# AUGRU from step 88 on with both halves as one

## The chip, the cores and the metric

The kernel runs on one core of a Trainium2 chip. The metric is the device time of one execution in microseconds, as the median of several runs. Engines are named as in the profile: PE (TensorE) multiplies matrices, PEld is its loading of weights, DVE (VectorE), ACT (ScalarE), POOL (GpSimd), and SP issues most of the transfers.

## The reference

A model of a recommender for 1024 users with a history of 100 items, 128 numbers each. A first GRU runs over the history, attention over its states gives weights, and a second GRU with an attention gate (AUGRU) runs over the same states. A small network then scores the user. All is float32.

```python
def augru_step(h, inp):
    x_t, a_t = inp                      # state of the first GRU, attention weight
    ti = jnp.concatenate([h, x_t], axis=-1)
    r = jax.nn.sigmoid(ti @ aug_Wr.T + aug_br)
    u = jax.nn.sigmoid(ti @ aug_Wu.T + aug_bu)
    h_hat = jnp.tanh(jnp.concatenate([h * r, x_t], axis=-1) @ aug_Wh.T + aug_bh)
    u = a_t[:, None] * u
    h_new = (1.0 - u) * h + u * h_hat
    return (h_new, h_new)
_, aug_seq = jax.lax.scan(augru_step, h0, (jnp.swapaxes(keys, 0, 1), att_seq))
...
idx = (sequential_length - 1)[:, None, None]   # lengths 1 to 100
attention_feature = jnp.take_along_axis(aug_out, idx, axis=1)[:, 0, :]
comb = jnp.concatenate([user, item, hist_sum, item * hist_sum, attention_feature], axis=1)
scores = _mlp(comb, layers, jax.nn.sigmoid)    # 640 -> 200 -> 80 -> 1
```

Only the state at a user's own last step is used, so a user whose history has ended need not be carried on.

## The kernel before

The first phase (GRU, attention, pooling) takes about 1400 us and is not touched. Users are then sorted by length, longest first, and dealt out to two halves of 512 columns (`NH = 2`, `HB = 512`). A state is held as 128 features by columns. In the second phase (`augru_phase`) step t works on the first `widths[t]` columns of each half alone: a planned bound on the users still alive (`ALIVE`), but never under `LEAST`, which is 96. The program holds this phase three times, for three plans of widths; a number computed on the chip chooses one. With the inputs here it is the first, whose bound falls from 512 to 14 columns: 100 at step 82, 96 at 83, 90, 86, 80, 76 at 84 to 87, then 70, 64, 60, 54, 50, 44, 40, 34, 28, 24, 18, 14. So before the change all steps from 83 on have 96 columns in each half.

The order of all engines' work is written out by hand (`manual_schedule`); each engine takes its instructions in that order. The two halves alternate: `half_step(t, i)` does one step of one half, and while one half waits for its gates the other fills the engines.

- `open_gates` starts the three sums of the next half step, `pr`, `ph` and `pu`, with their products with the key (the first GRU's state, L1110). `close_gate` ends each with its second product: `pr` and `pu` with the state `h`, `ph` with `r` (L1114). Each product appears in the profile as two MATMUL instructions with a weight load each.
- ACT makes the sigmoids of `pr` and `pu` in place (L1134, L1135) and the tanh of `ph` into `c` (L1122).
- DVE makes `r = h * pr` (L1140), `pu = pu * at` (L1148, `at` is the row of attention weights, the same in all partitions), `rest = (pu - 1) * h` (L1151), `pu = pu * c` (L1138) and the new state `h = pu - rest` (L1142). It also transposes the keys of two steps ahead in blocks of 32 columns (L1099, `load_key`).
- SP loads the attention rows two steps ahead (`load_att`, six tiles).
- POOL gathers the key rows of eight steps at a time, in the order of the sorted users.
- `predict(g)` is a job that scores the 64 users per half of group g once they have all ended. It goes forward one stage in each half step: two products of a prepared part and four of the state (L1200, L1205), two sigmoids (L1227), two products (L1233), a sigmoid (L1238), a product (L1241), a sigmoid (L1244). Group 1 (columns 64 to 127) falls due at step 88 and runs four steps later; group 0 is `final`, after the last step.

PSUM has seven banks that the sums take in turn (`ring`).

Of the kernel before, what the change touches and what calls it, by code (L numbers as in the profile page):

```python
# [9 lines left out]
F32 = mybir.dt.float32  # L10
# [3 lines left out]
AF = mybir.ActivationFunctionType  # L14
ALU = mybir.AluOpType
# [4 lines left out]
P = 128  # L20
B = 1024
T = 100
HB = 512
NH = B // HB
# [3 lines left out]
R = 32  # L28
# [4 lines left out]
MC = 100  # L33
# [26 lines left out]
GATHER = 70  # L60


EIGHTH, LEAST = 8, 96

LINES = (((0, 2, 38), (16, 8, 41)), ((0, 40, 41),))
ROOM = [
# [8 lines left out]
PR = P // NH  # L75
# [5 lines left out]
def kernel(ctx: ExitStack, tc: tile.TileContext, a: dict, out: bass.AP):  # L81
# [26 lines left out]
    nc = tc.nc  # L108
    const = ctx.enter_context(tc.tile_pool(name="const", bufs=1))
# [27 lines left out]
    idx = const.tile([P, GH, NH * 2], I32, name="idx")  # L137
    idx_k = const.tile([P, KH, NH], I32, name="idx_k")
    idx_p = const.tile([P, HB // PR], I32, name="idx_p")
    h3 = [const.tile([P, HB], F32, name=f"h3_{i}") for i in range(NH)]  # L140
    mid = ctx.enter_context(tc.tile_pool(name="mid", bufs=2))


# [1 line left out]
    later = {}  # L145
# [839 lines left out]
    def augru_phase(pools, widths, alive):  # L985
# [6 lines left out]
        sp = pools.enter_context(tc.tile_pool(name="sp3", bufs=2))  # L992
        kp = pools.enter_context(tc.tile_pool(name="kp3", bufs=4))

        ps = [
            pools.enter_context(tc.tile_pool(name=f"ps3_{n}", bufs=1, space=PSUM))
            for n in range(7)
# [8 lines left out]
        def bank(name, n=None):  # L1006

            if n is None:
                n = ring.pop(0)
                ring.append(n)  # L1010
            return ps[n].tile([P, HB], F32, tag="g", name=name)
# [63 lines left out]

        def load_att(t, i):
            w = widths[t]
            at = wp.tile([P, HB], F32, name="at", bufs=6)
            nc.sync.dma_start(
                out=at[:, :w], in_=att_d[i][t, :w].partition_broadcast(P)  # L1080
            )
            att[t, i] = at

        def load_key(t, i, n=None):

            q = max(j for j, first in enumerate(FIRST) if first <= t)
            w, m, r = widths[t], t - FIRST[q], rows[q, i]
            k = qp.tile([P, HB], F32, name="k3")
            if q < WHOLE:
                p = pa.tile([P, HB], F32, tag="a", name="pk3") if n is None else bank("pk3", n)  # L1090
                for g in range(-(-w // P)):
                    nc.tensor.transpose(p[:, ts(g, P)], r[:, g, ts(m, P)], ident)
                nc.scalar.copy(k[:, :w], p[:, :w])
            else:
                w, n = -(-w // R), KH // len(r)
                for j, part in enumerate(r):
                    u = min(w - j * n, n)
                    if u > 0:
                        nc.vector.transpose(  # L1099
                            k.rearrange("p (k r) -> p k r", r=R)[:, j * n : j * n + u, :],  # L1100
                            part[:, :u, ts(m, R)],
                        )
            keys[t, i] = k

        def open_gates(t, i, banks=(None,) * 3):

            k = keys.pop((t, i))[:, : widths[t]]
            for m, name, n in zip((wr, wh, wu), ("pr", "ph", "pu"), banks):
                p = opened[t, i, name] = bank(name, n)[:, : widths[t]]
                nc.tensor.matmul(p, lhsT=m[:, 1, :], rhs=k, start=True, stop=False)  # L1110
# [6 lines left out]
        def open_state(t, i):  # L1117

            r, u, rest = resets.pop((t, i))
            ph = close_gate(t, i, "ph", wh, r)  # L1120
            c = wp.tile([P, HB], F32, name="c3")[:, : widths[t]]
            nc.scalar.activation(c, ph, AF.Tanh, bias=later["bh"])  # L1122
            states[i] = u, c, rest, h3[i][:, : widths[t]]

        def half_step(t, i):


            w, h = widths[t], h3[i][:, : widths[t]]
            before, after = ((t - 1, 1), (t, 1)) if i == 0 else ((t, 0), (t + 1, 0))
            if before in resets:  # L1130
                open_state(*before)
            pr = close_gate(t, i, "pr", wr, h)
            pu = close_gate(t, i, "pu", wu, h)
            nc.scalar.activation(pr, pr, AF.Sigmoid, bias=later["br"])  # L1134
            nc.scalar.activation(pu, pu, AF.Sigmoid, bias=later["bu"])  # L1135
            state = states.pop(1 - i, None)
            if state is not None:
                nc.vector.tensor_mul(state[0], state[0], state[1])  # L1138
            r = wp.tile([P, HB], F32, name="r3")[:, :w]
            nc.vector.tensor_mul(r, h, pr)  # L1140
            if state is not None:
                nc.vector.tensor_sub(state[3], state[0], state[2])  # L1142
            if t == 1 and i == 0:
                store_weights(0, pa.tile([P, HB], F32, tag="a", name="pw"))
                first_state(1, spare)
            elif t == 1:
                first_weights(1, spare)
            nc.vector.tensor_mul(pu, pu, att.pop((t, i))[:, :w])  # L1148
            rest = wp.tile([P, HB], F32, name="rest")[:, :w]

            nc.vector.scalar_tensor_tensor(  # L1151
                out=rest, in0=pu, scalar=1.0, in1=h, op0=ALU.subtract, op1=ALU.mult
            )
            later["pace"] = rest[:, 0:1]
            resets[t, i] = r, pu, rest
            if after[0] < T and (*after, "pr") not in opened:
                open_gates(*after)
            if t == 1 and i:
                store_weights(1, spare)
            if t + 2 < T:  # L1160
                load_att(t + 2, i)

            if t == FIRST[1] - 1:
                load_key(t + 1, i)
            if FIRST[1] - 2 < t < T - 2:
                load_key(t + 2, i)

        def last_state(i):
            u, c, rest, h = states.pop(i)
            nc.vector.tensor_mul(u, u, c)  # L1170
            nc.vector.tensor_sub(h, u, rest)

        def predict(g, last=False):
# [36 lines left out]
                    stop=i == NH - 1,  # L1210
                )

            if last:
                for j in range(n):
                    of_part(j)
                for i in range(NH):
                    for j in range(n):
                        of_state(j, i)
                    yield
            else:  # L1220
                for j in range(n):
                    of_part(j)
                    for i in range(NH):
                        of_state(j, i)
                yield
# [38 lines left out]
        def last_places():  # L1264
            own = sp.tile([P, 1], F32, name="own3", bufs=1)
            nc.gpsimd.tensor_copy(own, idx_p[:, 0:1])
            later["places"] = []
            for i in range(NH):
                row = wp.tile([P, HB], F32, tag="att_r", name="places", bufs=2)
                nc.gpsimd.iota(  # L1270
                    row,
                    pattern=[[1, HB]],
                    base=i * HB,
                    channel_multiplier=0,
                    allow_small_or_imprecise_dtypes=True,
                )
                nc.gpsimd.tensor_scalar(row, row, own, None, ALU.is_equal)
                later["places"].append(row)
# [47 lines left out]
        more = gather_more()  # L1326
        jobs, final = [], None
        for t in range(1, T):
            if t + 1 in FIRST[1:-1]:
                all_of(ahead)  # L1330
                ahead, due = gathers(FIRST.index(t + 1) + 1), spread(FIRST.index(t + 1) + 1)
            for i in range(NH):
                half_step(t, i)
                for _ in range(due.pop(0) if due else 0):
                    next(ahead, None)
                if t > FIRST[1]:
                    next(more, None)
                if t == FIRST[2]:
                    store_weights(i, pa.tile([P, HB], F32, tag="a", name="pw"), R, T)

                for n, job in enumerate(list(jobs)):
                    job[0] += 1
                    if n == 0 and job[0] > 2 * G and next(job[1], job) is job:
                        jobs.remove(job)
            left = alive[t + 1] if t + 1 < T else 0
            for g in range(1, HB // PR):
                if left <= g * PR < alive[t]:
                    jobs.append([0, predict(g)])
                    if left:
                        next(jobs[-1][1])  # L1350
            if t == T - G:
                final = predict(0, last=True)
                next(final)
            if t == HALF_TIME:
                last_places()
        for _, job in jobs:
            all_of(job)
        earlier_results()
        open_state(T - 1, 1)
        next(final)  # L1360
        last_state(1)
        all_of(final)

    with ExitStack() as pools, tc.manual_schedule():
# [80 lines left out]
```

## Time and profile before

| | |
|---|---|
| time, three runs | 2012.97 us median (2011.99 to 2013.1) |
| the profiled execution | 2013.1 us, span of its instructions 2011.3 us |
| busy PE, PEld | 1989.6 us (99%), 1008.0 us (50%) |
| busy DVE, ACT, POOL | 1683.1 us (84%), 943.9 us (47%), 1275.5 us (63%) |
| mean ns at 96 columns: matmul (one of two) | 275, of `ph` with `r` 298 |
| sigmoids `pr` and `pu`, tanh | 307, 315, 341 |
| `r`, `pu * at`, `rest`, `pu * c`, `h` | 255, 255, 257, 266, 251 |
| transpose of a key | 268 |

Busy time is the union of an engine's instructions, and instructions overlap in it: the next one of an engine starts before the one ahead has ended. So the pace of an engine is read from the starts in the timeline, and a hop from one engine to another from the start of one instruction to the start of the one that waits for it. The ends of matmuls are modelled.

### The profile page before, as it was taken

What the parts mean: (1) busy time and instruction counts of PE and PEld (TensorE: products, weight loads), DVE (VectorE), ACT (ScalarE), POOL (GpSimd) and SP (SyncE); (2) the same over time, 40 slices, a digit from 0 to 9 for tenths busy, and PEclk for the clock granted to TensorE, in tenths of its full rate; (3) what the DMA queues carried; (4) which work ended last, traced back from release to release, by engine and by line L of the source; (5) the groups of instructions that cost most, each with busy time, mean ns of one, the idle gap of its engine ahead of it and who ended that gap; (6) DMA issues with size and microseconds to landing.
All of it is one profiled execution on the core that took longest, in us unless ns stands there. A gap on an engine that the chain in (4) does not pass through costs nothing.

```text
span 2011.3 us, 41368 instructions
## 1 busy us (share of the span) xinstructions
PE 1989.6 (99%) x15484; PEld 1008.0 (50%) x15484; DVE 1683.1 (84%) x3070; ACT 943.9 (47%) x1708; POOL 1275.5 (63%) x1327
## 2 busy tenths in 40 slices
PE   9999999999999999999999999998999999999998
PEld 2334444444444444444444444434444556678998
DVE  7878999887978887888878898998577777888987
ACT  4444454454444454444444454453434444445555
POOL 0233939569796959495887868898774454444331
PEclk9999999999999999999999999999999999999999
DMA  4443333323434434333333333333443333333332
GB/s 124 98 117 91 107 103 103 92 82 105 115 113 102 120 105 122 115 109 105 107 100 98 107 99 100 107 95 106 114 127 101 94 111 95 95 100 94 88 80 44
DMA packets 242174, 205.82 MB, mean 102 GB/s; under 512 B 59538, under 2 KB 204922, under 8 KB 241962
## 3 DMA queue, kind: packets, MB, share of 16 engines
q1 hardware_dynamic: 227514, 170.04, 30.6%
q0 software_dynamic: 12576, 32.31, 5.8%
q8 instruction: 124, 2.03, 0.4%
q10 hardware_dynamic: 1872, 0.72, 0.1%
q14 instruction: 88, 0.72, 0.1%
HBM read 146.95 MB, written 54.41 MB: 100 GB/s over the span
## 4 chain that ended last, share of the span: by engine, by line
PE 96%; DVE 2%; issue 1%; ACT 1%; DMA 0%; ACTq 0%; DVEq 0%
PE ps L530 49%; PE pm L696 17%; PE ph L1114 5%; PE pr L1114 5%; PE pu L1110 5%; PE pu L1114 5%; PE ph L1110 5%; PE pr L1110 5%; PE p L1205 0%; PE p L1233 0%; PE p L1200 0%; PE pd L239 0%; DVE ps L560 0%; DVE ps L567 0%; DVE d L566 0%
## 5 line engine op out<-in xcount | busy, mean ns | idle before, releaser
L530 PE MATMUL ps<-x,wih 128*32 128x512 f32 x4800 | 617.7, 593 | 0.0
L530 PE MATMUL ps<-hn,whh 128*32 128x512 f32 x4752 | 611.3, 592 | 0.9 <-ACT hn L578 0.9
L530 PEld LDWEIGHTS ps<-x,wih 128*32 128x32 f32 x4800 | 218.0, 110 | 300.9 <-issue 297.6
L530 PEld LDWEIGHTS ps<-hn,whh 128*32 128x32 f32 x4752 | 216.2, 110 | 296.7 <-issue 293.5
L515 POOL TENSOR_TENSOR xm<-x,m 128x512 f32<-128x512 f32 x200 | 234.3, 1171 | 143.6 <-DMA m<-mask_d 143.3
L542 ACT ACTIVATE r<-ps,brz 128x512 f32<-128x512 f32 x200 | 137.7, 688 | 387.5 <-PE ps L530 387.2
L516 POOL TENSOR_TENSOR hist<-hist,xm 128x512 f32<-128x512 f32 x200 | 258.3, 1291 | 15.7
L184 POOL DMA_INDIRECT rows<-keys_d,idx_k x220 | 213.3, 970 | 81.6 <-POOL rows L183 73.5
L633 POOL TENSOR_TENSOR pooled<-pooled,kw 128x512 f32<-128x512 f32 x191 | 245.3, 1284 | 15.0
L632 POOL TENSOR_TENSOR kw<-kt,e 128x512 f32<-128x512 f32 x191 | 206.0, 1078 | 69.7 <-DVE e L805 69.6
L561 ACT ACTIVATE ps<-ps,bih 128x512 f32<-128x512 f32 x200 | 132.4, 662 | 229.0 <-DVE ps L560 229.0
L1122 ACT ACTIVATE c<-ph,bh 128x96 f32<-128x96 f32 (+41 forms) x198 | 96.5, 488 | 275.5 <-PE ph L1114 275.4
L696 PE MATMUL pm<-hn,wk 128*32 128x512 f32 x1200 | 222.1, 592 | 0.0
L696 PE MATMUL pm<-kq,wkq 128*32 128x512 f32 x1200 | 222.0, 592 | 0.0
L550 DVE SCALAR_TENSOR_TENSOR u<-ps,bhh,r 128x512 f32<-128x512 f32 x198 | 147.5, 745 | 71.1 <-PE ps L530 68.3
L696 PE MATMUL pm<-mv,w 128*32 128x512 f32 (+1 forms) x808 | 195.4, 592 | 0.6 <-DVE e L786 0.6
L565 DVE TENSOR_TENSOR d<-hn,ps 128x512 f32<-128x512 f32 x198 | 136.0, 687 | 35.9 <-ACT ps L561 35.7
L560 DVE TENSOR_TENSOR ps<-ps,u 128x512 f32<-128x512 f32 x200 | 140.0, 700 | 25.9 <-remote 4.5
L578 ACT COPY hn<-ps 128x512 f32<-128x512 f32 x200 | 116.5, 583 | 93.1 <-DVE kq L572 91.4
L566 DVE TENSOR_TENSOR d<-ps,d 128x512 f32<-128x512 f32 x200 | 138.3, 692 | 25.9 <-ACT ps L562 11.4
L1138 DVE TENSOR_TENSOR pu<-pu,c 128x96 f32<-128x96 f32 (+41 forms) x197 | 88.3, 448 | 79.1 <-ACT c L1122 74.9
L183 POOL COPY rows<-rest 128x1 f32<-128x1 f32 x204 | 38.8, 190 | 175.6 <-DVE rest L1151 169.7
(191 smaller groups left out, 3214.1 us busy)
## 6 DMA issues: line engine op xcount, KB each, us to landing
x<-in_hist_x SPq DMA_DIRECT2D x210, 256.0 KB
keys_d<-kt SPq DMA_DIRECT2D x48, 1024.0 KB
m<-mask_d SPq DMA_DIRECT2D x200, 128.0 KB
rows<-keys_d,idx_k POOLq DMA_INDIRECT x220, 3.1
s_b<-mv SPq DMA_DIRECT2D x200, 8.0 KB
keys_d<-kt SPq DMA_DIRECT2D x32, 64.0 KB
at<-att_d SPq DMA_DIRECT2D x34, 48.0 KB
mask_i<-in_mask SPq DMA_DIRECT2D x8, 200.0 KB
```

What stands on the lines that cost most here:

```text
L184: nc.gpsimd.indirect_dma_start(out=r[:, at, :], out_offset=None, in_=keys_d[q], in_offset=bass.IndirectOffsetOnAxis(ap=idx_k[:, k, i : i + ...
L515: nc.gpsimd.tensor_mul(d, x, m)
L516: nc.gpsimd.tensor_add(acc, acc, d)
L530: nc.tensor.matmul(p[ts(q, R), :], lhsT=w[:, g, ts(q, R)], rhs=v, start=(j == 0), stop=(j == len(parts) - 1),)
L550: nc.vector.scalar_tensor_tensor(out=u, in0=ph, scalar=bhh[:, 2:3], in1=r, op0=ALU.add, op1=ALU.mult,)
L560: nc.vector.tensor_add(pi, pi, u)
L566: nc.vector.tensor_mul(d, pz, d)
L632: eng.tensor_mul(d, k, w)
L633: eng.tensor_add(acc, acc, d)
L696: nc.tensor.matmul(p[i][s, :], lhsT=w[:, s], rhs=v, start=start, stop=stop)
L1110: nc.tensor.matmul(p, lhsT=m[:, 1, :], rhs=k, start=True, stop=False)
L1114: nc.tensor.matmul(p, lhsT=m[:, 0, :], rhs=v, start=False, stop=True)
```

## The change

From the first step whose width is at most `ONE` = 72 columns, which is step 88, both halves are worked as one. `LEAST` falls from 96 to 32, so steps 84 to 99 go down to the planned bound, 32 at the least; the two halves together have 140 columns at step 88 and 64 from step 96 on. The two states become two parts of one tile, `h_all`. Keys and attention rows of both halves go into one tile at steps 88 and later.

In `whole_step` the products of the new state with the weights of `pr` and `pu` are split. The state is `c - rest`, where `c` is now `pu * c`; the sums of the next step first get the product of `rest` with the negated weights (`minus`) and are closed by the product with `c`. The subtraction that gives `h` itself is issued after that; it is needed for the next `r` and `rest`. The negated weights are made once, on POOL, at step 50.

On PE a whole step then has, in order: `pr` and `pu` with `c`, the keys' products of `pr` and `pu` of the next step, `ph` with `r`, the key's product of `ph` of the next step, `pr` and `pu` of the next step with `rest`; before the change two half steps have `ph`, `pr`, `pu` and three products with keys each. On DVE: the subtraction, a transpose, `r`, `pu * at`, `rest`, a transpose, `c`. The job `predict` goes forward two stages after each whole step.

```diff
-EIGHTH, LEAST = 8, 96
+EIGHTH, LEAST = 8, R
+ONE = 72
...
-    h3 = [const.tile([P, HB], F32, name=f"h3_{i}") for i in range(NH)]
+    h_all = const.tile([P, NH, HB], F32, name="h_all")
+    h3 = [h_all[:, i, :] for i in range(NH)]
...
+        minus = [wp.tile([P, P], F32, name=f"minus{j}", bufs=1) for j in range(2)]
+        one = min((t for t in range(T) if widths[t] <= ONE), default=T)
+        sums = {}
...
+        def both(tile, w, step=None):
+            step = step or w
+            return tile[:, : NH * step].rearrange("p (i w) -> p i w", i=NH)[:, :, :w]
+
+        def open_both(t, *names):
+            w = widths[t]
+            for name in names:
+                p = opened[t, name] = bank(name)
+                m = {"pr": wr, "ph": wh, "pu": wu}[name]
+                nc.tensor.matmul(
+                    both(p, w), lhsT=m[:, 1, :], rhs=both(keys[t, 1], w, P),
+                    start=True, stop=False,
+                )
+
+        def add_both(t, name, m, v, stop):
+            w = widths[t]
+            nc.tensor.matmul(
+                both(opened[t, name], w), lhsT=m, rhs=v[:, :, :w], start=False, stop=stop
+            )
+
+        def whole_step(t):
+            w = widths[t]
+            h = h_all[:, :, :w]
+            last = sums.pop(t - 1, None)
+            if last is None:
+                add_both(t, "pr", wr[:, 0, :], h, True)
+                add_both(t, "pu", wu[:, 0, :], h, True)
+            else:
+                c, rest, old = last
+                add_both(t, "pr", wr[:, 0, :], c, True)
+                add_both(t, "pu", wu[:, 0, :], c, True)
+                nc.vector.tensor_sub(old, c, rest)
+            pr, pu = (both(opened.pop((t, name)), w) for name in ("pr", "pu"))
+            nc.scalar.activation(pr, pr, AF.Sigmoid, bias=later["br"])
+            nc.scalar.activation(pu, pu, AF.Sigmoid, bias=later["bu"])
+            if t + 1 < T:
+                open_both(t + 1, "pr", "pu")
+            if t + 2 < T:
+                load_key(t + 2, 0)
+            tile = wp.tile([P, HB], F32, name="r3")
+            r = both(tile, w)
+            nc.vector.tensor_mul(r, h, pr)
+            nc.vector.tensor_mul(pu, pu, both(att.pop((t, 1)), w, P))
+            later["pace"] = tile[:, 0:1]
+            rest = both(wp.tile([P, HB], F32, name="rest"), w)
+            nc.vector.scalar_tensor_tensor(
+                out=rest, in0=pu, scalar=1.0, in1=h, op0=ALU.subtract, op1=ALU.mult
+            )
+            add_both(t, "ph", wh[:, 0, :], r, True)
+            c = both(wp.tile([P, HB], F32, name="c3"), w)
+            nc.scalar.activation(
+                c, both(opened.pop((t, "ph")), w), AF.Tanh, bias=later["bh"]
+            )
+            if t + 1 < T:
+                open_both(t + 1, "ph")
+                add_both(t + 1, "pr", minus[0], rest, False)
+                add_both(t + 1, "pu", minus[1], rest, False)
+            if t + 2 < T:
+                load_key(t + 2, 1)
+                for i in range(NH):
+                    load_att(t + 2, i)
+            nc.vector.tensor_mul(c, pu, c)
+            sums[t] = c, rest, h
...
             for i in range(NH):
-                half_step(t, i)
+                if t < one:
+                    half_step(t, i)
+                elif i == 0:
+                    whole_step(t)
...
+                for m, to in zip((wr, wu), minus):
+                    nc.gpsimd.tensor_scalar_mul(to, m[:, 0, :], -1.0)
```

Ahead of step 88 the second half's step 87 is finished first (`open_state`, `last_state`), and the closing job multiplies both halves' state in one product per part of the network instead of two.

## The prediction

> **What bounds the kernel now.** I read the page's busy table and its chain of waits first, then went to the stage that the change rewrites, the last 45 us, with the timeline, the groups by form and the windows.
>
> The page of the kernel before, busy time by engine and the chain that ended last:
>
> ```profile
> PE 1989.6 (99%) x15484; PEld 1008.0 (50%) x15484; DVE 1683.1 (84%) x3070; ACT 943.9 (47%) x1708; POOL 1275.5 (63%) x1327
> ...
> PE 96%; DVE 2%; issue 1%; ACT 1%; DMA 0%; ACTq 0%; DVEq 0%
> ```
>
> PE is the bound of the whole, so what counts in steps 88 to 99 is how many products PE issues and whether it ever waits. One half step at 96 columns, from the timeline (start, duration, engine, line):
>
> ```profile
> 1969.39 0.43 PE L1114 MATMUL ph<-r,wh 128*128 128x96 f32 x2
> 1969.66 0.39 PE L1114 MATMUL pr<-h,wr 128*128 128x96 f32 x2
> 1969.89 0.39 PE L1114 MATMUL pu<-h,wu 128*128 128x96 f32 x2
> ...
> 1970.10 0.31 ACT L1134 ACTIVATE pr<-pr,br 128x96 f32<-128x96 f32 x1
> 1970.11 0.39 PE L1110 MATMUL pr<-k,wr 128*128 128x96 f32 x2
> 1970.33 0.39 PE L1110 MATMUL ph<-k,wh 128*128 128x96 f32 x2
> 1970.44 0.26 DVE L1140 TENSOR_TENSOR r<-h,pr 128x96 f32<-128x96 f32 x1
> 1970.56 0.39 PE L1110 MATMUL pu<-k,wu 128*128 128x96 f32 x2
> 1970.78 0.43 PE L1114 MATMUL ph<-r,wh 128*128 128x96 f32 x2
> ```
>
> From product to product PE takes 0.22 us, and from one `ph` to the next 1.39. Six products are 6 x 0.2235 = 1.34; the other 0.05 is the `ph` product, which comes 0.27 before its successor instead of 0.22 because its weights were held back until `r` (1970.44 + 0.26) was there. So the half step is both nearly full on PE and tied into a loop: `r`, `ph` of one half, behind it in PE's order `pr` of the other, its sigmoid, its `r`. A whole step is 2.775.
>
> The kernel's end shows the same hops with nothing of the other half in the way:
>
> ```profile
> 2002.26 0.31 ACT L1134 ACTIVATE pr<-pr,br 128x96 f32<-128x96 f32 x1
> ...
> 2002.60 0.26 DVE L1140 TENSOR_TENSOR r<-h,pr 128x96 f32<-128x96 f32 x1
> ...
> 2002.91 0.46 PE L1114 MATMUL ph<-r,wh 128*128 128x96 f32 x2 [0.48 <-DVE r L1140]
> ...
> 2003.41 0.34 ACT L1122 ACTIVATE c<-ph,bh 128x96 f32<-128x96 f32 x1 [0.56 <-PE ph L1114]
> ...
> 2003.78 0.27 DVE L1170 TENSOR_TENSOR pu<-pu,c 128x96 f32<-128x96 f32 x1 [0.30 <-ACT c L1122]
> 2004.15 0.26 DVE L1171 TENSOR_TENSOR h<-pu,rest 128x96 f32<-128x96 f32 x1
> ```
>
> These starts are the prices of the single chain that the change makes. Counting half steps back from here, step 88's second half begins its sigmoid at 1970.10 and step 99's at 2002.26: 32.16 us for 22 half steps. 22 x 1.3875 is 30.53; the other 1.63 is the `predict` job of one group of rows, seen as three long gaps of ACT, the first of them here:
>
> ```profile
> 1982.59 0.31 ACT L1134 ACTIVATE pr<-pr,br 128x96 f32<-128x96 f32 x1
> ...
> 1985.07 0.31 ACT L1134 ACTIVATE pr<-pr,br 128x96 f32<-128x96 f32 x1
> ...
> 1985.58 0.62 ACT L1227 ACTIVATE f<-p,c 100x128 f32<-100x128 f32 x2
> ```
>
> 2.48 instead of 1.39: six extra products cost 1.09 on PE; the next two cost 0.36, the last 0.17.
>
> **PE's load, and what it waits for instead.** Per step the change removes 12 products of one half and adds 8 over both: three with the key, `ph` with `r`, and `pr` and `pu` twice each (with `c`, and with `rest` times the negated weights). At up to 128 columns a product keeps the 0.2235 (8 x 0.2235 = 1.79), at 140 columns about 0.245 (the pace at 142, starts 1924.61, 1924.86, 1925.10), 1.96. Either is under a chain that can no longer interleave two halves, so PE stops being the bound and latency takes over. Per step at 96 columns over both halves, from the lines above: sigmoid to `r` 0.34, `r` to `ph` 0.31, `ph` to tanh 0.50, tanh to product with `c` 0.37, that product to `pr` 0.32 (as `r` to `ph`, an instruction 10 ns longer), `pr` to its sigmoid 0.50 if PE stood waiting as in the second of these rows, 0.44 if it did not (1969.66 to 1970.10). The subtraction leaves the ring: 0.37 that is now beside PE and ACT. Sum 2.34; with 0.44 in both places 2.22. I take 2.34, since with 8 products PE will stand waiting at both.
>
> Width: two ACT instructions change by 0.83 ns a column (0.345 at 142, 0.307 at 96), two of DVE by 1.02 (0.302 and 0.255), two matmuls by about 0.4 (279 ns at 128 columns, 247 at 64): 4.5 ns a column. Steps 88 to 98 have 140, 128, 120, 108, 100, 88, 80, 68, 64, 64, 64 columns, 32 fewer in sum than 11 x 96. So 11 x 2.34 - 0.14 = 25.6 us.
>
> Who else could hold the ring? The second way round: `pr` product, `pu` sigmoid (0.27 behind the first, 0.32 long), `pu` times attention (0.03 later), `rest` (0.36 behind it), product with `rest` (0.31), two products (0.49), next `pr`: 0.50 + 0.27 + 0.35 + 0.36 + 0.31 + 0.49 = 2.28. That is only 0.06 short of 2.34, and at 64 columns equal. DVE has seven instructions at 0.17 apart (1970.44 to 1970.61), 1.2 of 2.3; the key's transposes stand ahead of `r` and of the product with `c`, but each has a hole of over 0.5 there. The attention rows go into one tile per step, so their loads run six steps ahead instead of three and stay hidden; SP's order keeps them alone there. POOL's two scalings of weights lie at step 50, where POOL is about half busy (27 of 50 us between 1800 and 1850); in the way of a gather they would cost their own duration once, under 1 us. I take nothing.
>
> **The job in the new order.** It stays and loses its other half. Six products (1.09) stand between the products with `rest` and the next `pr`, where there is at most 0.06 of slack; the two sigmoids (0.62 together) stand on ACT ahead of the next step's first sigmoid. The first starts about 0.43 after the last of those products begins, so the pair ends some 0.4 after that sigmoid could have started: 1.45. Then 0.40 and 0.15. Sum 2.0, against 1.63; from 1.6 (all sigmoids hidden) to 2.4.
>
> **The edges.** Into step 88 nothing is lost: `pr` over both needs the second half's state, tanh to `pr` 0.37 + 0.37 + 0.31, then 0.50, 1.55 against the 1.62 now measured between that half's tanh (1968.48) and sigmoid (1970.10): gain 0.1. Steps 84 to 87 at 90, 86, 80 and 76 columns instead of 96: the loop of the half step falls by about 2.3 ns a column until PE's 1.34 stops it: 0.014, 0.024, 0.037, 0.047, twice each, 0.25 (between 0 and 0.4). Tail: five instructions and a matmul 32 columns narrower, 0.15.
>
> **Sum.** 32.16 - (25.6 + 2.0) = 4.56; with 0.1, 0.25 and 0.15 it is 5.1 us. The profiled execution took 2013.1 us (span 2011.3), 0.13 above the median of its three runs, 2012.97. 2013.1 - 5.1 = 2008.0 for that execution, 2007.9 for the median. If the ring were 2.22, 1.3 better; if 0.1 is lost in each step, 1.1 worse; job 0.4 either way. So this case alone lies between 2006.2 and 2009.4. The measurement can tell about 0.2% from no change, 4.03 us (2008.94): most of this case is beyond it, not all.
>
> **The clock.** PE's granted clock in four windows of 3.41 us (length, PE busy, PEld, DVE, ACT, POOL, clock):
>
> ```profile
> 1424.01:1427.42 3.41, 2.02 (x17) 1.55 (x16) 0.00 (x0) 1.15 (x2) 2.65 (x3) 1.00 0.10 14
> ...
> 2000.87:2004.28 3.41, 2.79 (x24) 2.48 (x23) 2.50 (x12) 1.75 (x7) 0.00 (x0) 1.00 0.02 5
> 2004.28:2007.69 3.41, 2.05 (x18) 1.34 (x18) 0.13 (x1) 1.25 (x4) 0.00 (x0) 1.00 0.00 0
> 2007.69:2011.10 3.41, 0.36 (x7) 0.00 (x0) 0.42 (x1) 0.00 (x0) 0.00 (x0) 0.50 0.00 1
> ```
>
> After the third window the clock is halved, though no gap of PE in it reached 0.5 us. Streaming a column takes 0.84 ns a pass (a 362-column product of two passes every 0.61): that window streamed for about 0.30 of its time, the first, after which the clock stayed, for 0.44. The new steps stream 16 passes: 0.60 of a step at 108 columns, 0.39 at 64. The last four steps lie between the two windows.
>
> The Trainium skill (TensorE: Matmul & The Clock Gate, table of Part 1) ties the drop to an idle window of about 3.4 us, by which these steps would keep the clock and 2007.9 stands; the same page, section "A second HAM failure mode: psum-queue depth-cycling", reports drops from frequent micro-idling, which speaks against this change and agrees with the third window. By that the time would be the next rival's.
>
> **The rivals.** *The clock halves in the last steps.* Then a step is bound by PE, 8 x 0.447 + 0.05 = 3.63 instead of 2.16. The first window wholly within the steps from 95 on ends on average 5 us into their 11, some 2.7 steps before the end: + 4, and 2012 (2010 to 2014). For it: 0.39 is nearer to 0.44 than to 0.30 but below both windows that kept the clock; against it: PE's weight loads go on. 0.15.
>
> *The new ring does not shorten as counted*, because the way through `rest` or a second wait of an instruction (`r` and the product with the attention row now have two or three) holds it by 0.15 to 0.3 a step: 11 x 0.22 = 2.5 lost, 2010.4 (2009.5 to 2011.5). For it: 0.06 of slack; against it: the product with the attention row (L1148) waits for a DMA and for ACT already and starts 0.17 behind its predecessor. 0.17.
>
> *Slower: the clock halves from about step 91 on.* Nine steps at 3.63 instead of about 2.25 are 12.4 us more, 2020. It decides when the share of streaming that loses the clock is above 0.55; each step so lost costs 1.4 and four of them eat the gain. Against it stands the first window, which kept the clock at 0.44. 0.08, with whatever else would lengthen twelve steps so much.
>
> **How the numbers follow.** The forecast case has 0.60 and its time, 2007.9, is the prediction; about nine tenths of it is faster by over 0.2%. The two milder rivals are within 0.2%. So faster 0.54, same 0.38, slower 0.08. The range takes the forecast's own, the second rival and the lower half of the first: 2006.2 to 2012.2.
>
> **What would show it.** In the profile after: steps 90 and later of the new kind 2.4 us falling to 2.2 between sigmoids of `pr`, about 2.0 more around the job, PE busy near 0.8 there with gaps ahead of `ph` and of `pr` with `c`, released by DVE. The clock row at 1.00 up to the tail shows the rivals wrong; half rows before the tail show one right. Steps of 2.5 or more at 64 columns, or a ring that runs through `rest`, would make the forecast wrong.

## The result, and the profile after

The changed kernel takes 2008.85 us, median of 22 runs (2007.21 to 2013.23); beside it the kernel before takes 2012.55, median of 22 (2010.71 to 2014.85). The ratio is 0.9984, 95% interval [0.9979, 0.9990]: 3.7 us less by the medians, 3.2 by the ratio. The forecast was 2007.9 in a range from 2006.2 to 2012.2. The gain is real, and a little under the 0.2% that the prediction set as its bound.

The single times go with the mean granted clock of PE: the runs at 0.996 and 0.997 took 2007.2 to 2008.9, those at 0.992 and 0.993 took 2011.1 to 2013.2. The profiled execution stands between, 2009.0 us at 0.995, with a span of 2007.1.

The page of the kernel after, busy time by engine and the chain that ended last:

```profile
PE 1983.7 (99%) x15380; PEld 994.6 (50%) x15380; DVE 1671.7 (83%) x3010; ACT 934.8 (47%) x1672; POOL 1274.2 (63%) x1325
...
PE 28%; DVE 0%; ACT 0%; DMA 0%; issue 0%; ACTq 0%; DVEq 0%
```

PE has 104 instructions fewer and is 5.9 us less busy, DVE 11.4. The chain could be followed back through 28% of the span only, so the steps have to be read in the timeline. One new step at 64 columns in the kernel after (start, duration, engine, line; the ring's six hops and the next sigmoid, with the product of `rest`):

```profile
1992.10 0.29 ACT L1223 ACTIVATE pr<-pr,br 128x64 f32<-128x64 f32 x1 [0.84 <-PE pr L1204]
...
1992.42 0.22 DVE L1231 TENSOR_TENSOR r<-h_all,pr 128x64 f32<-128x64 f32 x1 [0.53 <-ACT pr L1223]
...
1992.69 0.43 PE L1204 MATMUL ph<-r,wh 128*128 128x64 f32 x2
...
1993.17 0.31 ACT L1240 ACTIVATE c<-ph,bh 128x64 f32<-128x64 f32 x1 [0.58 <-PE ph L1204]
1993.24 0.43 PE L1204 MATMUL pr<-rest,minus 128*128 128x64 f32 x2
...
1993.51 0.23 DVE L1251 TENSOR_TENSOR c<-pu,c 128x64 f32<-128x64 f32 x1 [0.21 <-ACT c L1240]
...
1993.79 0.43 PE L1204 MATMUL pr<-c,wr 128*128 128x64 f32 x2
...
1994.33 0.29 ACT L1223 ACTIVATE pr<-pr,br 128x64 f32<-128x64 f32 x1 [0.85 <-PE pr L1204]
```

0.32 + 0.27 + 0.48 + 0.34 + 0.28 + 0.54 = 2.23: the ring as it was forecast, and the product of `rest` 0.55 ahead of the one of `c`, so the second way round doesn't hold it. The tail and the clock are where the account differs. Windows of the same kernel (length, busy time and instructions of PE, PEld, DVE, ACT, POOL, then the granted clock, the DMA share and GB/s):

```profile
1989.00:1992.41 3.41, 3.38 (x29) 3.19 (x28) 1.87 (x10) 1.38 (x6) 1.97 (x2) 1.00 0.01 0
1992.41:1995.82 3.41, 3.36 (x26) 3.01 (x26) 1.97 (x10) 1.30 (x5) 0.00 (x0) 1.00 0.29 68
1995.82:1999.24 3.42, 3.14 (x14) 2.61 (x14) 1.50 (x7) 0.89 (x3) 0.00 (x0) 0.50 0.00 0
```

The clock is halved from 1995.82 to the end, from within step 98, and by the busy column nothing distinguishes the window that lost it from the one before. Before the change the clock held until 2007.69, after the closing job's large products; now these run at half pace (a timeline, kernel after, and the last row of the kernel before):

```profile
1996.81 0.29 ACT L1223 ACTIVATE pr<-pr,br 128x64 f32<-128x64 f32 x1 [1.10 <-PE pr L1204]
...
1999.02 1.18 PE L1304 MATMUL p<-h_all,m 128*100 128x128 f32 x4
...
2002.45 0.26 ACT L1343 ACTIVATE y<-p,c 128x1 f32<-128x1 f32 x1 [0.68 <-PE p L1340]
```

```profile
2006.89 0.26 ACT L1244 ACTIVATE y<-p,c 128x1 f32<-128x1 f32 x1 [0.47 <-PE p L1241]
```

From the sigmoid of step 99 (1996.81; 2002.26 before) to that of the scores it takes 5.64 us, 4.63 before, and SP's last instruction ends 10.26 after it instead of 9.0. The account of the two profiled executions (span 2011.3 to 2007.1, 4.2 us): 1.04 lies ahead of step 84, where the steps are unchanged, and is taken for a difference between executions; 0.33 on the way from step 84 to 88; 4.08 between the sigmoids of steps 88 and 99 (28.08 against 32.16), of which the half-clock end of the last step took back 0.25; and 1.25 is lost in the tail.

### The profile page after: what moved, and what is told of

Read it like the earlier page. It is cut to its first block, busy times and chain, and to the rows that moved or that the text cites. A ratio compares the mean times of both kernels' runs of the same rounds, so it can differ in the third digit from the quotient of the medians.

```text
span 2007.1 us, 41031 instructions
## 1 busy us (share of the span) xinstructions
PE 1983.7 (99%) x15380; PEld 994.6 (50%) x15380; DVE 1671.7 (83%) x3010; ACT 934.8 (47%) x1672; POOL 1274.2 (63%) x1325
## 5 line engine op out<-in xcount | busy, mean ns | idle before, releaser
L1139 ACT ACTIVATE c<-ph,bh 128x510 f32<-128x510 f32 (+57 forms) x174 | 88.3, 507 | 261.1 <-PE ph L1131 261.0
L571 DVE TENSOR_TENSOR ps<-ps,d 128x512 f32<-128x512 f32 x200 | 139.9, 700 | 6.8
```

What stands on the lines that cost most here:

```text
L571: nc.vector.tensor_add(pi, pi, d)
```

## The experiments

Theory 1: PE's clock is halved when the columns that stream through it fill too little of a 3.41 us window; at 64 columns the new steps lie at the edge of that, and the clock goes in their last windows or in the tail. Rivals: the tail's own waits lose it; it is an accident of the execution; or the time is elsewhere (theory 2 of the expectations: the ring, the split, the widths). The experiments ran in three comparisons, two on the chip that the record numbers 4 and the last on chip 6; the record names no chip for the result. The kernel before takes 2021.1 to 2021.9 us in them, against 2012.55 in the result; so they are read by ratios, and against the changed kernel, which ran once on each of the two chips.

**The changed kernel again** (no edit, first on chip 4, then on chip 6).

> The changed kernel itself, on the same chip as the next. Theory 1 (PE's clock halves in the last steps): its mean granted clock is lower than before's in most executions and its time spreads over 4 us and more; about 3.5 us under before. Theory 2 (the ring is longer than counted): as fast as fill_again within 0.5 us.

> The changed kernel once more, beside the three fillings on the same chip. Theory 1: slower than the fillings of the steps by 3 to 4 us, with a granted clock of 0.991 to 0.995 against 0.996 and over; ratio to the kernel before 0.9985 to 0.9995. Rival (the difference between the two earlier runs of it came from the chip alone): within 1 us of the fillings.

Measured: 2019.12 (11 runs, 2015.1 to 2021.1), 0.9991 [0.9982, 1.0], and 2018.88 (11 runs, 2016.08 to 2020.73), 0.9984 [0.9975, 0.9993]. The first gain, 2.2 us, is at the edge of the noise and less than the 3.5 expected. The two profiles show the same instructions with the clock lost at different places. In the first it held until 1.9 us behind step 99's sigmoid, and the way from step 88's sigmoid to step 99's took 27.83 us. In the second it went at the end of step 96; windows of it (columns as before):

```profile
1974.13:1977.55 3.42, 1.51 (x14) 1.37 (x13) 1.58 (x9) 0.75 (x3) 0.95 (x1) 1.00 0.41 107
1977.55:1980.96 3.41, 3.41 (x18) 3.36 (x17) 1.80 (x7) 1.08 (x4) 0.00 (x0) 0.50 0.07 15
...
1998.03:2001.44 3.41, 3.38 (x28) 3.16 (x28) 2.04 (x11) 1.36 (x5) 1.65 (x2) 1.00 0.01 0
2001.44:2004.85 3.41, 3.41 (x18) 3.41 (x18) 1.25 (x6) 0.89 (x4) 0.32 (x1) 0.50 0.28 67
```

A window with PE busy for 3.38 of 3.41 us lost it, and 28 instructions of PE became 18. The next steps took 3.28 and 3.41 instead of 2.23: eight products at 0.427, PE without a gap. The first two rows show a second place, the entry to step 88, where PE waits: one window lost, and a step of 3.32 instead of 2.58. Of the seven profiles on these chips with the same entry (this kernel's two, the fillings without products there, and the joined halves with 64 columns) four lost a window there.

**Products without use in PE's waits.** They multiply the identity matrix with itself (128 columns) into columns of PSUM that nothing reads.

```diff
+        def fill(t, name):
+            if FILL <= t < T:
+                p = early[t, name] = bank(name)
+                nc.tensor.matmul(
+                    p[:, HB // 2 : HB // 2 + P], lhsT=ident, rhs=ident, start=True, stop=True)
...
                 open_both(t + 1, "pr", "pu")
+                fill(t + 1, "ph")
...
                 add_both(t + 1, "pu", minus[1], rest, False)
+                fill(t + 2, "pr")
... (in predict, where last, at five places)
+                keep_warm()
```

Filling the steps that lead to 94 and later (`FILL = 94`), with the closing job (twice) and without it:

> Adds two products of constants (128 columns) to each step from 93 on, in the two places where PE waits, and five to the tail; nothing reads them. Theory 1 (PE's clock halves in steps 95 to 99 or at the start of the tail, in nearly every execution, and that takes back about 2 us): the streaming share of a 64-column step rises from 0.39 to 0.58, the clock stays at 1.00 up to the last product, the median falls to 2006.9 (2006.2 to 2007.8) and the runs lie within 1.5 us of each other. Theory 2 (the ring of a step is simply longer than counted, the clock matters little): the products delay the ring by up to 0.05 a step, 2009 to 2009.5.

> As fill_both without the five products of the tail. Theory 1: the steps keep the clock, the tail's last part loses it in some executions as in the kernel before: 2007.5 (2006.8 to 2008.3), so 0.5 more than fill_both. Theory 2: 2009 to 2009.5, as fill_both.

> The kernel of fill_both. Theory 1: 5.5 us under before (4.5 to 6.5) and about 2 under the changed kernel on this chip, spread smaller. Theory 2: no faster than the changed kernel.

With both: 2015.1 (11 runs), 0.9973 [0.9964, 0.9982], and in the second comparison 2015.15 (8 runs, 2013.94 to 2016.57), 0.9974 [0.9964, 0.9985], 4.0 us less than the changed kernel beside it (2 were expected). The runs spread over 4.7 and 2.6 us, where 1.5 was expected. Steps alone: 2016.8 (11 runs), 0.9978 [0.9969, 0.9987], 1.7 us over the filling of both beside it (0.5 expected; the intervals overlap). In the profiles with both fillings the clock is full from step 94 to the end (repeat) and to 1.1 us from it (first); with the steps alone it goes 5.0 us behind step 99's sigmoid.

The closing job alone:

> The changed kernel with five products without use (128 columns of the identity) in the waiting places of the closing job alone; nothing is added to the steps. Theory 1 (PE's clock halves when its columns stream too small a part of a window of 3.4 us, and the last steps at 64 columns are already under that part): the clock is lost in steps 97 to 99 or right behind them in most executions as without the products, and products that come after the loss run at half pace; no better than the changed kernel by more than 1 us: ratio to the kernel before 0.9985 to 0.9992 where the changed kernel has 0.999. Rival (only the closing job's own waits lose the clock): as good as with both fillings, 0.9974.

Measured: 2019.15 (11 runs), 0.9982 [0.9973, 0.9991], as the changed kernel beside it (2018.88). Its profile loses the clock at 2000.08, at the end of step 96, and steps 97 and 98 take 3.40 and 3.41. So the rival that the tail's waits alone are the cause falls: they can lose the clock, as in the kernel before and the first repeat, but here it was gone two steps earlier.

Filling only towards steps 97 to 99, the closing job, and three products in the wait at the entry to step 88; and the same with the filling from 94 on:

```diff
             if last is None:
+                p = bank("warm")
+                for _ in range(3):
+                    nc.tensor.matmul(p[:, :P], lhsT=ident, rhs=ident, start=True, stop=True)
```

> Filling in the waiting places of the steps that lead to 97, 98 and 99 alone, in the closing job, and three products at the entry to step 88, ahead of the first products of the whole steps (a wait of 1.0 to 2 us on PE). Theory 1, with a part between 0.39 and 0.45 that keeps the clock: steps 94 to 96 at 68 and 64 columns (0.39 to 0.41) are too few to fill a window of their own, so the clock holds, and the 0.4 us that the earlier filling cost in steps 93 to 96 come back: 0.3 to 1 us better than the filling from 94 on, ratio 0.997. Rival (the part needed is nearer to 0.45, or the windows lie badly): clock lost in some executions, 0.9975 to 0.9985.

> Filling of the steps from 94 on and of the closing job as before, and three products at the entry to step 88 in addition. Theory 1: where a window with that entry in it lost the clock for 3.4 us (one profile so far, a step of 3.32 instead of 2.58), it no longer does; in the mean 0 to 0.5 us better than without the three products, ratio 0.997 to 0.9975, and step 88's entry no longer, since the products lie in PE's wait for the second half's state. Rival (the products at the entry stand in the way of step 88's): 0.3 to 0.7 us slower than without them.

Measured: 2016.33 (8 runs, 2015.53 to 2018.15), 0.9973 [0.9962, 0.9983]; and 2016.93 (8 runs), 0.9974 [0.9963, 0.9984]; every one of these 16 executions has a mean clock of 0.996 or 0.997, where the changed kernel beside them has 0.992 to 0.995. Windows of the lighter one:

```profile
1999.09:2002.50 3.41, 3.41 (x32) 3.39 (x31) 2.12 (x11) 1.29 (x6) 1.97 (x2) 1.00 0.18 25
2002.50:2005.92 3.42, 3.42 (x29) 3.19 (x28) 1.56 (x7) 1.10 (x5) 0.00 (x0) 1.00 0.15 49
2005.92:2009.33 3.41, 2.91 (x22) 2.48 (x22) 1.11 (x5) 1.32 (x5) 0.00 (x0) 1.00 0.00 0
```

The last of them lies in the tail, at full clock; SP's last instruction ends 8.65 after step 99's sigmoid, against 10.26. Step 99's sigmoid and that of the scores, 4.46 behind it:

```profile
2005.81 0.29 ACT L1234 ACTIVATE pr<-pr,br 128x64 f32<-128x64 f32 x1 [0.84 <-PE pr L1205]
...
2010.27 0.26 ACT L1366 ACTIVATE y<-p,c 128x1 f32<-128x1 f32 x1 [0.47 <-PE p L1361]
```

The difference between the two amounts of filling (0.6 us) is under what these runs can tell, and so is what the three products at the entry bring to the time; neither profile with them lost a window there. This lighter filling is a version that beats both kernels: 5.6 us under the one before, 2.5 under the changed one beside it (3 to 4 were expected).

A rival remains: on these chips the clock is also lost near 1434, at the start of the second phase, in four of the twelve profiles (both repeats and the joined halves with 96 and with 64 columns) and in none with a filling. In the first repeat this cost 3.0 us: it has 13.98 between two sigmoids of `pr` (1431.64 and 1445.62) where the second filling has 10.95 (1432.34 to 1443.29). So the 4.0 us of that pair needn't be the filling's alone. The filling of the closing job answers it: its profile has no such loss and begins step 84 at 1964.0, the lighter filling's at 1963.7, yet its median is 2.8 us higher (2019.15 against 2016.33). Of these two only the lighter one has products in the steps and at the entry. So, as far as one profile of each can tell, these 2.8 us belong to the clock from step 88 on.

**Narrower half steps alone**, without joining the halves (`LEAST` stays 32):

```diff
-ONE = 72
+ONE = 0
```

> Only the narrower widths: half steps to the end, 90 down to 32 columns in each half, no step with both halves as one. Theory 1: PE issues 12 passes a half step and streams 12 x 0.84 ns a column: 0.45 of the time at 60 columns, 0.38 at 50, 0.24 at 32, so the clock halves from about step 92 or 93 on and a half step bound by weight loads goes from 1.34 to 2.68: about 14 of them, 2028 (2020 to 2032), slower than before. Theory 2: 32 half steps at 1.34 instead of 1.39, 2011.

Measured: 2042.01 (4 runs, 2034.7 to 2050.65), 1.0099 [1.0068, 1.0131], 20 us slower, more than the 15.5 (7.5 to 19.5) expected. Windows of it:

```profile
1974.16:1977.57 3.41, 2.88 (x24) 2.59 (x24) 2.28 (x13) 1.93 (x8) 0.00 (x0) 1.00 0.27 67
1977.57:1980.99 3.42, 3.42 (x18) 3.42 (x18) 2.16 (x12) 1.26 (x5) 0.00 (x0) 0.50 0.11 23
```

The clock is gone from 1977.57 to the end at 2044.6. It went in a window that holds a stop of PE of 0.53 us (from 1974.36; see the last section), so the loss isn't shown to be the narrow products' own; that it doesn't return in 67 us is. Six products at 0.427 make half steps of 2.55 us where 96 columns at full clock took 1.39; and by theory 1, as fewer columns fill even less of a window, it never comes back. With the fillings this is the strongest evidence for it: the same products, less work in each, and nearly twice the time.

**Joined halves without narrowing** (96 columns in each half to the end) **and with 64:**

```diff
-EIGHTH, LEAST = 8, R
+EIGHTH, LEAST = 8, 3 * R          # the other kernel: 2 * R
...
-        one = min((t for t in range(T) if widths[t] <= ONE), default=T)
+        one = 88 if widths[88] <= LEAST else T      # in the first alone
```

> Whole steps from 88 on as changed, but at least 96 columns in each half, 192 in all: the two halves as one without the narrower widths. PE: 16 passes of 0.166, 2.65 a step. Ring: 2.34 at 96 columns and 4.5 ns a column more, 2.77, and the 0.1 by which the changed kernel's steps at 120 to 140 columns were over that count, 2.87. 11 steps and the job 33.2 us against 32.16 before: about 1 us slower than before, at most 2. Streaming 0.9, so the clock stays to the tail under both theories.

> Least width 64 instead of 32, so 128 columns over both halves from step 89 on; the rest as changed. Theory 1: 16 passes of 128 columns stream for 0.66 of a step, the clock stays; 11 steps of 2.57 (as measured at 128 columns) and 1.65 for the job make 29.9 us between the sigmoids of steps 88 and 99, 2.1 more than the 27.8 of the changed kernel at full clock: 2009.0 (2008.3 to 2009.8), a narrow spread. So wider would be no slower than the changed kernel, which loses as much to the clock. Theory 2: 2.1 above the changed kernel's 2008.85, 2011.

With 96: 2023.48 (10 runs), 1.001 [1.0001, 1.002], 2.2 us slower, a little more than expected. Its steps are 3.02 at 192 columns (2.87 expected) against two half steps of 1.39, and the clock holds up to 3.1 us from the end. With 64: 2017.18 (11 runs), 0.998 [0.9971, 0.9989]. Its steps are 2.57 where the changed kernel has down to 2.23, yet it is no slower than the changed kernel in its two comparisons (0.9991, 0.9984). A narrow spread was expected of it, but its runs go from 2016.27 to 2022.01; the slowest is the profiled one, which lost the clock near 1434 and at the entry as well as in the tail. Joining was a gain only with narrow steps; narrow steps alone were a loss; and the last narrowing, from 128 to 64 columns, bought nothing that these runs can tell. Theory 1 has the reason: the clock took back what the ring gave.

**State not split** (`pr` and `pu` closed with `h` after the subtraction, no products of `rest`: six products a step):

```diff
+                nc.vector.tensor_sub(old, c, rest)
-                add_both(t, "pr", wr[:, 0, :], c, True)
-                add_both(t, "pu", wu[:, 0, :], c, True)
-                nc.vector.tensor_sub(old, c, rest)
+                add_both(t, "pr", wr[:, 0, :], h, True)
+                add_both(t, "pu", wu[:, 0, :], h, True)
...
-                add_both(t + 1, "pr", minus[0], rest, False)
-                add_both(t + 1, "pu", minus[1], rest, False)
```

> Whole steps as changed, but pr and pu are closed with the state itself: the subtraction is ahead of them, the products with rest and the negated weights are gone, six products a step. By the ring: 0.37 more a step, 4.4 us in 12 steps, which leaves about 1 us over before if the clock stays. Theory 1: 12 passes stream for 0.44 of a 120-column step of 2.8 us and for 0.25 at 64, so the clock halves from about step 91 on, and each of the ring's two matmul hops grows by some 0.3: 5 us more, 6 over before (3 to 9). Theory 2: 1 over before.

Measured: 2028.44 (5 runs), 1.0033 [1.002, 1.0047], 7.1 us slower. Its clock is gone from 1977.44, the window with the entry's wait, to the end, so its steps (3.39 at 64 columns) are steps at half clock throughout, with PE waiting for `h` in each (timeline, `pr` of a step at 64 columns):

```profile
2008.63 0.69 PE L1204 MATMUL pr<-h_all,wr 128*128 128x64 f32 x2 [0.57 <-DVE h_all L1219]
```

The two products of `rest` do two things, then: they take the subtraction out of the ring, and they are columns that help to keep the clock or bring it back (the second repeat lost a window at the same entry and recovered). How much of the 9 us against the changed kernel is the first isn't separated; no step of this kernel ran at full clock.

## Why the prediction was right, and where it was off

**The bound** was read rightly: the ring of six hops, not PE, sets the whole steps at full clock, down to 2.23 at 64 columns. The sign given for it, PE busy near 0.8 with gaps, didn't show: PE counts as busy for 3.38 of 3.41 us, with no gap ahead of `ph` or of `pr` with `c`, and the ends of matmuls are modelled. It is the starts that show the ring. (The 0.245 taken as PE's pace for 140 columns stands in rows of 146; nothing rested on it.)

**The ring**: 25.6 for eleven steps was forecast. In the repeat that kept the clock, 27.83 less 1.63 for the job is 26.2, 0.05 a step over. Steps of 140, 128 and 120 columns took 2.57, 2.57 and 2.58 against 2.54, 2.48 and 2.45: 4.5 ns a column, taken from rows of 64 to 142 columns, was about right up to 100 columns (2.41 at 100, 2.23 at 64). In the two runs with products at the entry the steps of 128 and 120 took 2.51 and 2.46, so the excess there isn't the width alone; its cause is open. The second rival (0.22 a step) is refuted at that size, and the way through `rest` holds nothing.

**The job**: 2.0 was forecast, from 1.6 to 2.4; 1.63 measured, as much as before the change: against the ring at these widths the three steps are 1.23, 0.31 and 0.09 longer, where 1.45, 0.40 and 0.15 were counted. The pair of sigmoids in the timeline after:

```profile
1984.40 0.63 ACT L1326 ACTIVATE f<-p,c 100x128 f32<-100x128 f32 x2 [1.60 <-PE p L1291]
1984.91 0.30 ACT L1223 ACTIVATE pr<-pr,br 128x80 f32<-128x80 f32 x1
```

The step's own sigmoid follows 0.51 behind the start of the pair, as the prediction had it: the pair on ACT stands ahead of it. What the job cost less (0.4) and the ring more (0.6) nearly cancel.

**The edges** ahead of step 88: 0.35 forecast, 0.33 measured.

**The tail and the clock** are the step that failed. The tail was counted as 0.15 of gain; it cost 1.25 in the profiled execution, since the clock was lost 12 us earlier than before the change (1995.82 against 2007.69). At full clock it is a gain of 0.35 (8.65 against 9.0, with the fillings). The prediction had the mechanism as its first rival: a threshold between streaming shares of 0.30 and 0.44, and 0.39 for the last steps. What it had wrong was to put it at 0.15, as something that happens to an execution or not. The threshold lies so near the steps' own share that it happens to most executions, at another window in each: 14 of the 22 have a mean clock of 0.995 or less, and the profiled one, at 0.995, lost it in step 98. Against a tail at full clock (8.65) the price is 1.4 us where only the tail is lost (first repeat, 10.01) and 3.8 where the last two steps go with it (second repeat: 1.05, 1.18 and 1.61). A step at half clock cost 3.41, not 3.63, so its price was 1.18 and not 1.47. With the clock kept, the forecast's account holds: the executions at 0.997 took 2007.2 to 2007.9. That the median lies in the range is in part luck: the range reached up for a rival held unlikely, and by the prediction's own sign, a half clock row ahead of the tail, that rival is what the profiled execution shows. Seven of the 22 took 2010 us or more, that rival's range, and two of them are above the forecast's.

**The slower rival** (a threshold above 0.55) is refuted for this change; a clock at half from then on is what made the half steps alone and the unsplit state slower.

## What to carry to other kernels

Before making a product narrower, work out what part of each 3.4 us its columns stream: below a certain part (here 0.36 to 0.39) a PE without a gap lost half its clock, and a few products without use were then worth their time. Where one part of a change removes work from PE and another makes it wait, try the parts alone: here each alone was slower than nothing, the joining by 0.1%. A latency ring could be priced to 0.05 us a step from rows in which its instructions stand alone; a tail has to be priced with the clock that the steps ahead leave it.

## What the runs showed of the hardware

**The streaming share that keeps the clock.** I counted, in the traces of 14 profiles, passes times columns times 0.84 ns in each window, on the grid of 3.41 us on which the clock changes (in the profile after it changes at 1401.90, 1412.14 and 1995.82, 3 and 171 times 3.413 apart), from the second phase on and up to the closing job, whose products have other shapes. Of windows at full clock, none above 0.39 was followed by half clock and none below 0.36 by full. In between both occur: 0.38 kept it twice in the first repeat, 0.38 lost it in the second, and in the profile after 0.38 was followed by 0.37, which lost it. Back from half clock it came after windows with 0.39 or more of such columns (reckoned at the full rate; two had 0.39, in the second repeat from 1434.83 and with 64 columns from 1436.89, the others 0.44 and more); with 0.38 or less it stayed, and so the narrow half steps (0.25 falling to 0.12, at most 0.32 with the job) never came back. Loading of weights seems not to count: PEld was busy for 3.16 of 3.41 us in a window that lost the clock. The share is worked out; that it is columns, and not something that goes with them, rests on the fillings and the narrow half steps.

The Trainium skill (TensorE: Matmul & The Clock Gate, table of Part 1) ties the drop to an idle window of about 3.4 us. The length of the window agrees with the grid here; idleness, as the profile counts it, doesn't, since PE was busy 3.36 to 3.38 us in windows that lost it.

**A stop of PE in the experiments' profiles.** There PE pauses for 0.3 to 0.7 us about every 20 us in the second phase (the first repeat: 1926.79, 1946.86, 1966.61; the profile shows no releaser for the first and the last), which the profiles before and after, taken for the result, don't show. In most a longer one falls into the entry to step 88. The tanh of step 87's second half, in the kernel after (the result's profile) and in the first filling (chip 4):

```profile
1967.18 0.32 ACT L1139 ACTIVATE c<-ph,bh 128x76 f32<-128x76 f32 x1 [0.58 <-PE ph L1131]
```

```profile
1973.97 0.32 ACT L1140 ACTIVATE c<-ph,bh 128x76 f32<-128x76 f32 x1 [1.50 <-PE ph L1132]
```

The wait for the same product is 0.92 us longer, and step 88 starts 3.6 after step 87's sigmoid instead of 2.7. The wait at the entry to step 88 is then long enough to cost a window its clock (the row at 1974.13 above, PE busy 1.51 of 3.42 us). What stops PE there is not settled, and whether the kernel before has these stops on chips 4 and 6 wasn't profiled.
